# A decoder layer's feed-forward: the second matrix, too, by Strassen's seven block products

## The chip, the cores and the metric

The kernel runs on one core of a Trainium2 chip. TensorE (PE) multiplies matrices out of SBUF into PSUM, which has eight banks of 128 x 512 float32. VectorE (DVE) and ScalarE (ACT) read PSUM and SBUF, GpSimd (POOL) only SBUF. SyncE (SP) issues most of the DMAs. Each engine works through its own instructions in order and waits on semaphores for the others. The metric is device time in microseconds (us) of one execution.

## The reference

All arithmetic is float32. x is 8 x 256 x 1024, that is 2048 tokens of 1024.

```
x = x + selfattention(layernorm(x))          # 32 heads, sign weights
x = x + crossattention(layernorm(x), ctx)    # 16 heads
h = layernorm(x)
P = h @ U1                                   # 1024 -> 256
H = P @ V1 + b1                              # 256 -> 2 x 2752
act = silu(H[:, :2752]) * H[:, 2752:]
Z = act @ U2                                 # 2752 -> 256
x = x + Z @ V2 + b2                          # 256 -> 1024
```

The change concerns Z = act @ U2; its neighbours in the program are V1 and V2.

## The kernel before, in words

The two attentions take the first 960 us or so. Then comes the feed-forward, for two halves of 1024 tokens (`dbs`: d0, then d1). Each half has two column blocks of W = 512 tokens (t = 0, 1), and everything is held transposed, features on partitions. The instructions are issued in the order of the program on every engine; nothing reorders them.

`Head` prepares 512 tokens: it loads x rows from DRAM, normalizes them (`norm`), stores them, loads them back (`take`), transposes them on DVE (`turn`) and multiplies by U1 (`factor`, PSUM tile ps_p, copied out by ACT). `sums` forms four combinations t1 to t4 of a half's P blocks on DVE. Heads 0 and 1 (d0) come during the last cross attention; heads 2 and 3 (d1) during d0's units.

The 2752 hidden features are 21 full chunks of 128 and one of 64. `unit` (L1176) does one chunk for a whole half: gate and up parts of 128 features by two column blocks, that is a 2 x 2 by 2 x 2 block product, done with Strassen's seven products (Winograd's form) in place of eight. Its sums of V1 blocks (s_) come from `weight_sums` (L1151) on POOL, one unit ahead. The products go into three PSUM tiles, c21, c11 and c12. c21 gathers four products, and ACT copies it out between them (a1, q, q7). DVE adds and multiplies with scalar_tensor_tensor (`stt`), ACT takes the sigmoids, POOL does three multiplications. The results are g1 and ac2, the activations of that chunk for t = 0 and 1. The last steps of a unit (sigmoid sg2 and two POOL products, `rest`) are issued within the next unit, by `trailing`, and `mid` issues there what is due of other work (`todo`, filled by `at(unit, ...)`).

`down` (L1275) multiplies each chunk's activations by its rows of U2: four products of 128 x 128 by 128 x 512 per unit (two column blocks t, two halves r of the rank 256), all accumulated over the 21 chunks in four PSUM banks, zs (psA twice, psB, pso). They are queued in `zq` and `fill` puts them between the products of the next unit, as work that PE can do while it would wait. The 64-feature chunk is done by `half_unit` three units before the end, for both column blocks at once, and its U2 products by `across`. After the last chunk zs is copied to zT.

`tail` multiplies zT by V2 (PSUM tile ps_o, in two pieces of 512 columns per 128 tokens), adds the x rows on DVE and sends the result out; `tail_b` adds b2 to the x rows on POOL beforehand; `tail_x` loads them. The tail of d0 is spread over d1's units 1 to 8, that of d1 comes at the end. `tail_b` runs in d0's unit 20 and d1's units 1 to 7 for d0, and in d1's units 10 to 17 for d1.

The other four PSUM banks are one rotating pool, pss, which scores, c21, c11, c12, ps_h, ps_p of heads 2 and 3, and ps_o use.

## Time and profile before

| | |
|---|---|
| Median of 3 runs | 1477.05 us (1476.87 to 1477.11) |
| The profiled execution | 1477.6 us, its span 1475.8 us |
| PE busy | 1439.5 us, 98% of the span |
| DVE, ACT, POOL busy | 969.6, 853.1, 655.9 us |
| A unit of d0, from start to start | 9.52 us |
| The products c (L1189) | 588 records of 592 ns (634 for the fourth of c21), two to a product |
| The U2 products ps_z (L1285) | 336 records, 592 ns |
| POOL: L1231, L1232, L1215; L1156 to L1159; L1303 | 1.27 each; 0.455 each; 2.35 us |
| DVE: L1200, L1217, L1222, L1226; L1144; L1319 | 0.751 each; 0.692; 0.692 us |
| ACT: copies of c; sigmoids | 0.586; 0.63 us |

A line of the profile begins with a start and a duration, or with a source line. "c<-t,s_v" is an instruction that writes tile c from tiles t and s_v; buffer numbers are left out, so c21, c11 and c12 are all "c". PE records overlap: 592 ns is one from first to last element, and they start every 429 ns. PEld is the loading of weights. In square brackets stands how long an engine was idle before an instruction, and what ended that. In the row of slices each digit is the busy share of a fortieth of the span, in tenths.

### The profile page before, as it was taken

What the parts mean: (1) busy time and instruction counts of PE and PEld (TensorE: products, weight loads), DVE (VectorE), ACT (ScalarE), POOL (GpSimd) and SP (SyncE); (2) the same over time, 40 slices, a digit from 0 to 9 for tenths busy, and PEclk for the clock granted to TensorE, in tenths of its full rate; (3) what the DMA queues carried; (4) which work ended last, traced back from release to release, by engine and by line L of the source; (5) the groups of instructions that cost most, each with busy time, mean ns of one, the idle gap of its engine ahead of it and who ended that gap; (6) DMA issues with size and microseconds to landing.
All of it is one profiled execution on the core that took longest, in us unless ns stands there. A gap on an engine that the chain in (4) does not pass through costs nothing.

```text
span 1475.8 us, 25648 instructions
## 1 busy us (share of the span) xinstructions
PE 1439.5 (98%) x8986; PEld 960.4 (65%) x8986; DVE 969.6 (66%) x1894; ACT 853.1 (58%) x2557; POOL 655.9 (44%) x771
## 2 busy tenths in 40 slices
PE   6899999999999999989999999999999999999998
PEld 6778888888888887667777777644444344444433
DVE  6888898989898988767777777434424333333334
ACT  5778898989898988755555666433223222223320
POOL 2544444445454444312322264246645436657840
PEclk9999999999999999989999999999999999999999
DMA  8520020202020142344458674723212001230003
GB/s 230 114 58 17 29 71 18 73 16 73 16 73 21 39 131 93 115 118 131 133 149 281 203 226 148 224 72 121 86 43 89 25 1 61 82 125 33 0 0 114
DMA packets 102960, 134.74 MB, mean 91 GB/s; under 512 B 44538, under 2 KB 75440, under 8 KB 102704
## 3 DMA queue, kind: packets, MB, share of 16 engines
q1 hardware_dynamic: 98224, 116.33, 26.6%
q0 software_dynamic: 4608, 16.78, 2.9%
q8 instruction: 72, 1.18, 0.3%
q14 instruction: 56, 0.46, 0.1%
HBM read 90.60 MB, written 41.94 MB: 90 GB/s over the span
## 4 chain that ended last, share of the span: by engine, by line
PE 55%; ACT 2%; DVE 1%; DMA 1%; issue 0%; SPq 0%; ACTq 0%; DVEq 0%
PE c L1189 17%; PE ps_z L1285 10%; PE ps_pt L579 4%; PE s L676 4%; PE ps_o L1311 4%; PE ps_p L1123 4%; PE po L699 3%; PE ps_o L716 2%; PE ps_q L925 2%; PE ps_qk L941 2%; ACT p L762 2%; PE ps_k L855 1%; PE ps_o L547 1%; PE ps_h L1246 0%; DMA n<-xn 0%
## 5 line engine op out<-in xcount | busy, mean ns | idle before, releaser
L762 ACT ACTIVATE p<-s,nm 128x256 f32<-128x256 f32 x768 | 359.0, 519 | 3.3 <-DVE nm L743 3.3
L583 ACT COPY pT<-ps_pt 128x512 f32<-128x512 f32 x384 | 197.6, 599 | 145.9 <-PE ps_pt L579 145.8
L743 DVE TENSOR_REDUCE nm<-s 128x2 f32<-128x512 f32 x384 | 237.4, 678 | 5.2 <-PE s L676 3.7
L579 PE MATMUL ps_pt<-ident,p 128*128 128x128 f32 x1536 | 198.5, 281 | 5.9 <-DVE p L623 2.5
L579 PEld LDWEIGHTS ps_pt<-ident,p 128*128 128x128 f32 x1536 | 167.0, 142 | 46.5 <-issue 24.6
L762 ACT ACTIVATION_READ_ACCUMULATOR p<-s,nm 128x1 f32 x768 | 192.5, 251 | 0.0
L731 POOL TENSOR_TENSOR x1t<-x1t,y 128x256 f32<-128x256 f32 x64 | 46.3, 743 | 201.0 <-DVE y L724 201.0
L407 POOL TENSOR_SCALAR tmp<-y 128x512 f32<-128x512 f32 x78 | 58.5, 750 | 166.8 <-DVE y L556 91.6
L1217 DVE SCALAR_TENSOR_TENSOR ac<-c,b_col,q 128x512 f32<-128x512 f32 x42 | 31.5, 751 | 148.0 <-ACT q L1214 148.0
L1231 POOL TENSOR_TENSOR g<-g,sg 128x512 f32<-128x512 f32 x41 | 52.1, 1271 | 168.5 <-ACT sg L1230 168.5
L1195 ACT COPY a<-c 128x512 f32<-128x512 f32 x42 | 24.6, 586 | 169.1 <-PE c L1189 169.1
L1189 PE MATMUL c<-t,s_v 128*128 128x512 f32 x252 | 121.8, 592 | 0.0
L454 PE MATMUL ps_q<-xh,qT_w 128*128 128x256 f32 x496 | 121.8, 287 | 0.0
L454 PE MATMUL ps_q<-xl,qT_w 128*128 128x256 f32 x496 | 118.9, 281 | 0.0
L547 PE MATMUL ps_o<-oT_w,oh 128*128 128x512 f32 x256 | 106.5, 416 | 0.0
L547 PE MATMUL ps_o<-oT_w,ol 128*128 128x512 f32 x256 | 101.8, 398 | 0.0
L454 PEld LDWEIGHTS ps_q<-xh,qT_w 128*128 128x128 f32 x496 | 93.3, 188 | 1.7
L454 PEld LDWEIGHTS ps_q<-xl,qT_w 128*128 128x128 f32 x496 | 93.4, 188 | 0.0
L623 DVE TENSOR_SCALAR p<-p,sm 128x256 f32<-128x256 f32 x256 | 86.8, 396 | 8.4 <-PE ps_q L454 0.5
L630 ACT ACTIVATE p<-p,sm 128x256 f32<-128x256 f32 x172 | 75.9, 514 | 19.1 <-DVE sm L613 18.5
L1189 PEld LDWEIGHTS c<-t,s_v 128*128 128x128 f32 x252 | 47.7, 190 | 60.0 <-issue 57.6
L1285 PE MATMUL ps_z<-g,u_sb 128*128 128x512 f32 x168 | 85.3, 592 | 0.0
(185 smaller groups left out, 3038.2 us busy)
## 6 DMA issues: line engine op xcount, KB each, us to landing
xs<-in_x_dram SPq DMA_DIRECT2D x32, 512.0 KB
x<-xs POOLq DMA_DIRECT2D x16, 512.0 KB, 3.1
x1t<-x SPq DMA_DIRECT2D x16, 512.0 KB
c<-in_ctx_dram SPq DMA_DIRECT2D x64, 128.0 KB
n<-xn SPq DMA_DIRECT2D x32, 256.0 KB
xp<-n SPq DMA_DIRECT2D x64, 128.0 KB
x<-x1t POOLq DMA_DIRECT2D x16, 512.0 KB, 5.6
x2n<-x SPq DMA_DIRECT2D x16, 512.0 KB
```

What stands on the lines that cost most here:

```text
L454: nc.tensor.matmul(ps[:, i, :], w(i, e), x_[:, e, :], start=(e == 0 and x_ is st.xh), stop=(e == EC - 1 and x_ is st.xl),)
L547: nc.tensor.matmul(ps, o_[c // 4][:, c % 4, t * P : (t + 1) * P], oT_w[:, c, h * 512 : (h + 1) * 512], start=(c == 0 and o_ is st.oh), sto ...
L579: nc.tensor.transpose(ps[:, k, t * P : (t + 1) * P], p[:, t, k * P : (k + 1) * P], ident)
L583: nc.scalar.copy(pT, ps)
L623: nc.vector.tensor_scalar_mul(p, p, self.sm[:, t, j : j + 1])
L630: nc.scalar.activation(p, p, AF.Copy, scale=self.sm[:, t, j : j + 1])
L676: nc.tensor.matmul(s[2 * i + j][:, t, :], st.cqk[p0 : p0 + XD, 2 * c + i, t * P : (t + 1) * P], st.ckv[p0 : p0 + XD, :], start=True, stop= ...
L743: nc.vector.tensor_reduce(nm[:, j, :], s[j], AX.X, ALU.max, negate=True)
L762: nc.scalar.activation(cur.p[j][:, t, :], s[j][:, t, :], AF.Exp, bias=nm[:, j, t : t + 1], accum_out=cur.sm[:, t, j : j + 1],)
L1123: nc.tensor.matmul(ps, fw.u1[:, e, r * P : (r + 1) * P], self.chunk(e), start=(e == 0), stop=(e == EC - 1),)
L1189: nc.tensor.matmul(ps, w, x_, start=start, stop=stop, skip_group_check=True)
L1285: nc.tensor.matmul(db.zs[t][r], fw.u2[f // 4][:, f % 4, r * P : (r + 1) * P], ac, start=(k == 0), stop=last,)
```

## The change

Pairs of chunks (`pair`: chunks f1 and f2 of units 2p and 2p+1) form 2 x 2 blocks with the two column blocks and the two halves of the rank, and are multiplied with seven products (P1 to P7) in place of eight. Ten pairs cover 20 of the 21 chunks; the last one is multiplied as before (`left`). Four of the seven products are kept in PSUM over all pairs (keys "2", "3", "4" and "5" in the four banks that zs had). The other three (P1, P6, P7, key "1") go one after another into one bank, and DVE adds each to zT in SBUF (`more`). `finish` puts the sums together. DVE forms t1 and t2 (new tiles) and t3 and t4 (in place) from the activations; POOL forms four sums of U2 blocks in the place of zT[:, 0, 1, :] (`sums1`, `sums2`). A pair's products are issued in units 2p+2 (P1, P2, P5) and 2p+3 (P6, P3, P7, P4), at the places `jobs`, its other work at `also` and `sums_`.

The pool pss becomes four single banks with names of their own: c21 and c11 swap banks 0 and 1 from unit to unit (`flip`), c12 has bank 2, the key "1" tile bank 3. ps_p of heads 2 and 3 and the tails' first piece take the bank of the last c11 (`spare`), the tails' other pieces bank 2. Scratch tiles change their places. The last attention step's `weighted`, `early` and `late` move into d0's unit 0; `half_unit` moves from before unit 18 to before unit 20. Two norms and four turns of the heads now share a unit, on odd units; tails, their loads and `tail_b` move one or two units later.

```
-    pss = ctx.enter_context(tc.tile_pool(name="pss", bufs=4, space=PSUM))
+    pss = ctx.enter_context(tc.tile_pool(name="pss", bufs=1, space=PSUM))
...
-                ps = pss.tile([P, W], F32, tag="pss", name="ps_p")
+                ps = spare("ps_p")
...
+    def bank_(i, name):
+        return pss.tile([P, W], F32, tag=f"pss{i}", name=name)
+    def spare(name):
+        return bank_(1 - flip[0], name)
...
+        flip[0] ^= 1
+        c21 = bank_(flip[0], "c21")
         product(c21, v1_of(0, 0, f, P), b11, True, False)
         act(a1, c21)
+        c11 = bank_(1 - flip[0], "c11")
         product(c11, v1_of(1, 0, f, P), b21, True, True)
         trailing()
         stt(g1, c11, bg, a1, ALU.add, ALU.add)
         if mid is not None:
             mid()
-        fill(1 + (extra > 0))
+        do(jobs[0])
+        do(also[0])
         product(c21, s_[:, 1, :], db.t2, False, False)
         nc.scalar.activation(sg1, g1, AF.Sigmoid)
         act(q, c21)
+        c12 = bank_(2, "c12")
         product(c12, s_[:, 0, :], db.t1, True, False)
-        fill(1 + (extra > 1))
+        do(sums_[0])
+        do(jobs[1])
         product(c21, s_[:, 2, :], db.t3, False, False)
         act(q7, c21)
         mul(g1, g1, sg1)
         stt(ac2, c12, bu, q7, ALU.add, ALU.add)
         if following is not None:
             weight_sums(*following)
-        fill()
+        do(sums_[1])
+        do(jobs[2])
         product(c21, v1_of(1, 1, f, P), db.t4, False, True)
         stt(g1, c21, bu, g1, ALU.add, ALU.mult)
-        fill()
+        do(also[1])
+        do(jobs[3])
         product(c12, s_[:, 3, :], b22, False, True)
         stt(g2, c12, bg, q, ALU.add, ALU.add)
+        do(also[2])
...
+        def t1():
+            m.b11, m.b12 = db.ac[2 * p]
+            sub(m.t1, m.b12, m.b11)
+        def t23():
+            m.b21, m.b22 = db.ac[2 * p + 1]
+            sub(m.t2, m.b22, m.t1)
+            sub(m.b12, m.b22, m.b12)
+        def t4():
+            sub(m.b21, m.b21, m.t2)
+        def sums1():
+            m.s = db.zT[:, 0, 1, :].rearrange("p (k c) -> p k c", k=4)
+            nc.gpsimd.tensor_add(m.s[:, 0, :], u2_of(f1, 1), u2_of(f2, 1))
+        def sums2():
+            g.tensor_sub(m.s[:, 1, :], m.s[:, 0, :], u2_of(f1, 0))
+            g.tensor_sub(m.s[:, 3, :], u2_of(f2, 0), m.s[:, 1, :])
+            g.tensor_sub(m.s[:, 2, :], u2_of(f1, 0), u2_of(f1, 1))
+        def more(t, r):
+            dst = db.zT[:, t, r, :]
+            if p:
+                add(dst, db.X["1"], dst)
+            else:
+                nc.vector.tensor_copy(dst, db.X["1"])
+            if end and t:
+                add(dst, dst, db.zT[:, r, 0, :])
...
++        p1 = new(chain(lambda: u2_of(f1, 0), lambda: m.b11))
++        p2 = kept("2", lambda: u2_of(f2, 0), lambda: m.b21)
++        p5 = kept("5", lambda: m.s[:, 0, :], lambda: m.t1, end)
++        p6 = new(chain(lambda: m.s[:, 1, :], lambda: m.t2))
++        p3 = kept("3", lambda: m.s[:, 3, :], lambda: m.b22)
++        p7 = new(chain(lambda: m.s[:, 2, :], lambda: m.b12))
++        p4 = kept("4", lambda: u2_of(f2, 1), lambda: m.b21)
++        m.even = dict(jobs=([p1], [p2], [p5], []),
++            also=([lambda: more(0, 0), t23], [], [t4]), sums_=([sums1], [sums2]))
++        m.odd = dict(jobs=([p6], [p3], [p7, p4], []),
++            also=([lambda: more(1, 0)], [lambda: more(1, 1)], []))
...
+    def left(db, t, r):
+        down(db, KEYS[t, r], u2_of(units[FULL - 1], r), db.ac[FULL - 1][t], True)
+    def finish(db, *which):
+        for t, r in which:
+            if (t, r) == (0, 1):
+                add(z[0][1], db.X["4"], z[1][1])
+            else:
+                add(z[t][r], db.X[KEYS[t, r]], z[t][r])
+            if t:
+                add(z[t][r], db.X["5"], z[t][r])
...
-            ps = pss.tile([P, n], F32, tag="pss", name="ps_o")
+            ps = bank_((1 - flip[0], 2)[c0 // 512], "ps_o")[:, 0:n]
...
+            if k // 2 < FULL // 2:
+                a = e["also"]
+                e["also"] = (a[0] + [pairs[db.i, k // 2].t1_],) + tuple(a[1:])
...
         for j in range(1, 2 * BT):
-            at(j, tail_b, d0, j)
+            at(j + 1, tail_b, d0, j)
         for j in range(2 * BT):
-            at(2 * BT + j, last_x, j)
-            at(2 * BT + j + 2, tail_b, d1, j)
+            at(2 * BT + j + 2, last_x, j)
+            at(2 * BT + j + 4, tail_b, d1, j)
...
         trailing()
-        fill(2)
-        tail(d1, 0)
-        fill(len(zq))
-        for j in range(1, 2 * BT - 1):
+        end = pairs[1, FULL // 2 - 1].odd
+        for i in range(4):
+            for f in end["jobs"][i]:
+                f()
+            if i in (0, 2):
+                end["also"][i // 2][0]()
+        for c in range(2):
+            across(d1, c)
+        for t in range(2):
+            for r in range(RC):
+                left(d1, t, r)
+            finish(d1, *([(0, 0), (0, 1)] if t == 0 else [(1, 0), (1, 1)]))
+        for j in range(2 * BT - 1):
             tail(d1, j)
```

t1 of a pair is issued in unit 2p+1, at that unit's first `also` place. At d0's end `trailing`, P6 and its add come before the two factors of head 3; P3, P7 and P4 follow in d1's unit 0, and `across`, `left` and `finish` of d0 in d1's unit 1.

## The prediction

> **What bounds the kernel now.** I read the page's busy line first, then its slices, then the chain of waits in the feed-forward stage, and last the timeline of single units there.

> ```profile
> PE 1439.5 (98%) x8986; PEld 960.4 (65%) x8986; DVE 969.6 (66%) x1894; ACT 853.1 (58%) x2557; POOL 655.9 (44%) x771
> PE   6899999999999999989999999999999999999998
> POOL 2544444445454444312322264246645436657840
> ...
> by line: PE c L1189 48.0%; PE ps_z L1285 27.3%; PE ps_o L1311 14.0%; PE ps_p L1123 6.2%; PE ps_h L1246 1.8%; PE ps_z L1265 1.1%; DVE g L1226 0.2%; DVE g L1231 0.2%; DVE ac L1232 0.2%; ACT sg L1230 0.2%; DVE zT L1295 0.2%; DVE x2t L1319 0.1%
> 1116.50 0.94 PE c L1189 x2
> 1117.44 0.86 PE ps_z L1285 x2
> 1118.30 2.58 PE c L1189 x6
> ```

> PE never rests in the last 500 us: the chain there is PE work end to end. A matmul is two records of 0.429 us, so a product costs 0.857 us (a "slot"). A unit, from 1108.78 to 1118.30, takes 9.52 us: 7+4 slots are 9.43, and 0.09 is the 0.94 (for 0.86) of the fourth c21 product, which waits for the copy q7. So a slot removed is worth 0.857 us, if nothing that feeds PE comes later than before. What feeds it stands in one unit, which starts at 1366.46:

> ```profile
> 1366.46 1.02 PE L1189 MATMUL c<-pT,w_ffn 128*128 128x512 f32 x2
> 1367.52 0.59 ACT L1195 COPY a<-c 128x512 f32<-128x512 f32 x1 [3.79 <-PE c L1189]
> 1368.01 0.63 ACT L1230 ACTIVATE sg<-g 128x512 f32<-128x512 f32 x1
> 1368.71 1.27 POOL L1231 TENSOR_TENSOR g<-g,sg 128x512 f32<-128x512 f32 x1 [1.59 <-ACT sg L1230]
> 1370.06 1.27 POOL L1232 TENSOR_TENSOR ac<-ac,g 128x512 f32<-128x512 f32 x1
> 1371.29 2.36 POOL L1303 TENSOR_TENSOR x2t<-x2t,b_sb 128x1024 f32<-128x1024 f32 x1
> 1373.29 0.75 DVE L1217 SCALAR_TENSOR_TENSOR ac<-c,b_col,q 128x512 f32<-128x512 f32 x1 [4.09 <-ACT q L1214]
> 1373.59 1.28 POOL L1215 TENSOR_TENSOR g<-g,sg 128x512 f32<-128x512 f32 x1
> 1374.81 0.47 POOL L1156 TENSOR_TENSOR s_v<-w_ffn,v1b 128x128 f32<-128x128 f32 x1
> ```

> POOL starts 2.25 us into the unit, held by ACT (a, then sg); its two products of the unit before end at 4.83; the bias add of the tail (L1303, 2.35 us, in 16 units) ends at 7.13. Today nothing on PE waits for it.

> The next rows show what happens when DVE and POOL both work from SBUF:

> ```profile
> 966.48 0.99 DVE L1143 TENSOR_TENSOR t<-pT 128x512 f32<-128x512 f32 x1 [1.04 <-PE ps_p L1123]
> 966.88 0.90 POOL L1156 TENSOR_TENSOR s_v<-w_ffn,v1b 128x128 f32<-128x128 f32 x1
> ...
> 1433.33 0.69 DVE L1215 TENSOR_TENSOR g<-g,sg 128x512 f32<-128x512 f32 x1 [0.76 <-ACT sg L1206]
> 1433.43 1.71 POOL L1232 TENSOR_TENSOR ac<-ac,g 128x512 f32<-128x512 f32 x1
> 1443.14 3.70 PE L1311 MATMUL ps_o<-v_sb,zT 128*128 128x512 f32 x8 [1.90 <-DVE zT L1295]
> ```

> A DVE operation with two SBUF inputs and a POOL operation exclude each other: the subtraction of 966.48 took 0.99 (others 0.69), the POOL sum behind it 0.90 (others 0.455), and a POOL product of 1.27 took 1.71. The last line is PE's only real pause at the end, 1.90 us.

> **Gains.** (a) 10 pairs in each of two halves lose one product each: 20 x 0.857 = 17.1. (b) In odd units two products stand between q7's source and the fourth c21 product, so the 0.09 goes in 19 units (3 to 19 of each half, and d1's unit 1, which has z products there): 1.7. (c) In d0's unit 0 PE now has the 16 small matmuls of the last attention step between c11 and the next product, where it had a 0.68 pause; from the end of the factor (971.4) unit 0 takes about 9.0 where 10.05 passed until 981.42: 1.05. (d) The 1.90 pause above goes with the old end. Together 21.8.

> **What is added and hidden.** Three DVE adds from PSUM per pair (as L1319, 0.692) and four subtractions (as L1144, 0.692) are 4.9 us; DVE's four L1200/L1217/L1222/L1226 operations are 3.0 of 9.5 us a unit: room for them, if the moment suits. The four sums of u2 chunks on POOL (as L1156 to L1159, 0.455) are 1.8 us per pair. The reads of u2 chunks 4 and 5 and the loads of x rows move on SP behind unit 0 or by one unit: u2's are first used in unit 16, and each x row still has a unit or more between load and use. So nothing. Fixed banks for c21, c11, c12: each is read out 0.9 us or more before its next use. So nothing inside the units.

> **Losses.** In an even unit the slots start at: c21 0, c11 0.86, P1 1.71, c21 2.57, c12 3.43, P2 4.29, c21 5.14, P5 6.00, c21 6.86, c12 7.71, end 8.57 plus 0.09.

> 1. *P5 behind the bias add.* P5 needs the first u2 sum, which POOL's queue has behind the two products and, in 9 even units (d0's 20; d1's 2, 4, 6, 8, 12, 14, 16, 18), behind L1303. Without exclusion the sum ends at 7.13+0.46 = 7.59; PE follows a POOL result after 0 to 0.3 us (the handover is not shown cleanly; I take 0.27, as from the end of the POOL product at 980.30 to the matmul at 980.57): start 7.86 instead of 6.00, less the 0.09 that vanishes: 1.77 each, 15.9. With exclusion DVE's t2, which waits for the POOL product that ends at 4.87, asks at 4.90, just after L1303 has started; it runs 7.13 to 7.70, the sum 7.70 to 8.12, P5 at 8.4: 2.3, and 2.4 where an odd unit has left POOL late: 5 x 2.3 + 4 x 2.4 = 21.1.
> 2. *Odd units 13, 15, 17, 19 of d1.* POOL enters late (2.6 for 2.25), t1 waits for L1303's end (7.5), ac's scalar_tensor_tensor stands behind it on DVE, and the last c12 product behind that: 8.9 to 9.1 for 8.57. 0.5 each, 2.0; without exclusion 0. In d1's 3, 5, 7 the tail's 3.43 us of PE work let POOL catch up: 0.
> 3. *Even units without a bias add.* POOL: sum until 5.25, t2 until 5.80, then the product L1215, waiting since 5.25, until 7.03, then the next subtraction until 7.6; ac's operation ends 8.33 and the last c12 product starts 8.4 for 7.8: 0.6 in 8 units, 4.8. d0's unit 2 has inv_std (0.96) and two DMA issues (1.2 from 996.89 to 998.07) ahead of the sum: 1.7; unit 6 has inv_std (1.5): 1.1; d1's unit 20 has its products on DVE: 0.95. Together 8.55; without exclusion 2.0.
> 4. *Two norms (L1077) in one unit* (d0's 3, 5, 11, 13): each waits for a POOL product, as at 1102.60 (1.42), so the add that frees P7's bank ends at 6.55: P7 0.65 late, 2.6; with 0.55 each and no waiting 1.6. Two pairs of transposes (2.5) just fit: 0.
> 5. *Bank of the factor.* ps_p takes the bank that the next c21 (or the second factor) needs at once; ACT copies it out first: 0.2+0.59+0.05 = 0.85, four times: 3.4.
> 6. *d0's unit 1* has no product to fill: c21 waits for q (4.02 for 3.43) and q7 (5.73 for 4.88): 1.4.
> 7. *P6 behind d0's unit 20* waits for the second u2 sum, behind four sums of v1 chunks: 1.55; 1.0 without exclusion.
> 8. *End.* P7's bank waits for an add that DVE has behind sg2 and the two last products: start 13.3 us after unit 20's start for 11.3, 2.0. The last three pieces share one bank and wait for each other's add (0.65 and 0.5): 1.2. Together 3.2; the adds of z hide behind across and left (5.5 us).

> D1's unit 2 also has six adds of finish before its first DVE operation, but its P5 waits longer anyway.

> Losses 21.1+2.0+8.55+2.6+3.4+1.4+1.55+3.2 = 43.8; minus 21.8: 22 us slower. The profiled execution took 1477.6 (span 1475.8 and 1.8 around it), 0.04% above the median of 1477.05; I add to the median: 1499.

> [...]

> **Rivals.**
> - *No order from the exclusion* (subtractions slip in at no price): 15.9+0+2.0+1.6+3.4+1.4+1.0+3.2 = 28.5, minus 21.8: 1483.8. For it: only the few rows above and the norms show the wait. Against: each shows it.
> - *Worse queueing*: in units with a bias add, the POOL product overtakes the second subtraction as in step 3, so the last c12 product starts 0.7 later, 9 times, and odd units lose double (2 more): 1499+8.3 = 1507. The order at 8.12 decides it.
> - *Faster: the u2 sum is in time.* If P5 does not wait behind L1303, step 1 is 0; with the cheap values elsewhere 12.6 of losses against 21.8: 1468. It decides where P5's wait falls under 1.0 us in the nine units (9.2/9). Against it: POOL keeps its order, and in the rows above it is busy without a gap from 2.25 until past 7.13.

> **How the numbers follow.** 1499: 0.53; 1484: 0.21; 1507: 0.13; faster, about 1468: 0.13. The range 1481 to 1508 leaves out the last and the edges of the others. About 0.2% (3 us) is what a measurement of this kernel can tell from no change; 0.04 lies within it, at the near edge of the 1484 case: faster 0.13, same 0.04, slower 0.83. The likeliest case's own range is 1492 to 1505.

> **What would show it.** PE's weight load for P5 waiting for POOL sums in the nine units, about 2 us each; bias adds with DVE subtractions of 2 to 3 us beside them; ACT's ps_p copy releasing c21 four times; 20 products fewer (40 records); even units near 9.3 and odd near 9.4 where no bias add runs. Wrong if P5 has no wait, if even units run at 8.7, or if the end is waited out elsewhere.

## The result, and the profile after

| | before | after |
|---|---|---|
| Median, measured together | 1477.08 us (1476.87 to 1478.39) | 1496.98 us (1495.98 to 1497.75) |
| Ratio, 95% interval | | 1.0132 (1.0115 to 1.0150) |
| The profiled execution, its span | 1477.6, 1475.8 us | 1497.6, 1495.5 us |
| PE busy | 1439.5 us, 8986 matmul records | 1430.3 us, 8946 records |
| DVE, POOL busy | 969.6, 655.9 us | 1120.0, 723.3 us |
| Start of the last factor before d0's unit 0 (ps_p, 7.03 us) | 964.49 us | 960.77 us |
| From there to the end: "the stage" | 511.3 us | 534.7 us |

The change makes the kernel slower by 1.3%; 1499 was predicted. The instructions ahead of the stage are the same in both, yet they take between 960.8 and 965.2 us in the profiles of this case (the granted clock of TensorE stood at 0.92 to 0.97 between 600 and 700 us). So profiles are compared here by the stage: it takes 23.4 us more.

The page of the kernel after, its busy line and two rows of its slices (tenths of a fortieth of the span):

```profile
PE 1430.3 (96%) x8946; PEld 952.5 (64%) x8946; DVE 1120.0 (75%) x2046; ACT 849.6 (57%) x2553; POOL 723.3 (48%) x851
...
PE   7899999999999999899999999999999999998988
...
POOL 2544454445354534122232435177657646668950
```

The 40 records that are missing are the 20 products. PE is busy 9 us less, in a span 20 us longer; three of the last four slices show 8 tenths. Of DVE's 150 us more some 100 are the added instructions (4.9 us for each of 20 pairs); the rest is waiting that their records contain.

A unit with a bias add (d1's unit 12), in the timeline: start and duration in us, engine, line, operation, and in brackets the idle time before it and what ended that.

```profile
1352.56 1.02 PE L1189 MATMUL c<-pT,w_ffn 128*128 128x512 f32 x2
...
1356.22 1.27 POOL L1241 TENSOR_TENSOR ac<-ac,g 128x512 f32<-128x512 f32 x1
...
1357.44 2.35 POOL L1396 TENSOR_TENSOR x2t<-x2t,b_sb 128x1024 f32<-128x1024 f32 x1
1357.52 2.82 DVE L1302 TENSOR_TENSOR t<-ac,t 128x512 f32<-128x512 f32 x1 [1.50 <-POOL ac L1241]
...
1359.75 0.90 POOL L1310 TENSOR_TENSOR zT<-u_sb 128x128 f32<-128x128 f32 x1
1360.26 0.93 DVE L1303 TENSOR_TENSOR ac<-ac,ac 128x512 f32<-128x512 f32 x1
1360.61 1.71 POOL L1221 TENSOR_TENSOR g<-g,sg 128x512 f32<-128x512 f32 x1
...
1360.70 1.13 PE L1285 MATMUL z<-t,zT 128*128 128x512 f32 x2 [1.98 <-POOL zT L1310]
1361.12 0.74 DVE L1223 SCALAR_TENSOR_TENSOR ac<-c,b_col,q 128x512 f32<-128x512 f32 x1
```

Read it downwards: the bias add (L1396) starts as the second product (L1241) ends. DVE's t2 (L1302) asks 0.08 us later, and its record lasts 2.82 us, for 0.69 of work: it gets its turn when the bias add ends. Then POOL's first u2 sum (L1310) has its turn, then DVE's second subtraction (L1303), then POOL's product: they alternate, one operation each. P5 (the z of 1360.70) starts 0.05 us after the sum's end and 8.14 us into the unit, where its place is 6.00. PE had nothing for 1.98 us.

An even unit without a bias add (d0's 14):

```profile
1121.70 0.93 DVE L1302 TENSOR_TENSOR t<-ac,t 128x512 f32<-128x512 f32 x1 [1.50 <-POOL ac L1241]
...
1122.04 1.72 POOL L1221 TENSOR_TENSOR g<-g,sg 128x512 f32<-128x512 f32 x1
1122.55 1.75 DVE L1303 TENSOR_TENSOR ac<-ac,ac 128x512 f32<-128x512 f32 x1
...
1124.22 0.74 DVE L1223 SCALAR_TENSOR_TENSOR ac<-c,b_col,q 128x512 f32<-128x512 f32 x1
...
1125.02 1.13 PE L1189 MATMUL c<-pT,s_v 128*128 128x512 f32 x2 [0.31 <-DVE ac L1223]
```

The second subtraction waits for the POOL product beside it (1.75 us for 0.69), ac's operation stands behind it, and the last c12 product behind that: 9.24 us from unit start to unit start, for 8.66.

Something else took time that no step of the prediction has. The same d1 unit and its successor by stretches of 2 us; the columns are the busy time (and instructions) of PE, PEld, DVE, ACT and POOL, then the granted clock of TensorE:

```profile
1358.00:1360.00 2.00, 0.73 (x2) 0.00 (x0) 2.00 (x1) 0.58 (x1) 2.00 (x2) 1.00 0.00 0
1360.00:1362.00 2.00, 1.30 (x3) 0.68 (x4) 1.86 (x3) 0.00 (x0) 2.00 (x2) 1.00 0.00 0
1362.00:1364.00 2.00, 2.00 (x4) 0.80 (x3) 0.66 (x1) 0.00 (x0) 1.92 (x5) 0.50 0.00 0
1364.00:1366.00 2.00, 2.00 (x5) 0.81 (x4) 1.11 (x3) 0.00 (x0) 1.37 (x4) 0.65 0.00 0
```

Behind P5's wait the clock is halved for 3.4 us, and PE loses 1.7 us more: d1's unit 18, which holds such a stretch whole, takes 12.51 us where units 14 and 16 take 10.82. This document calls such a stretch a clock dip. There are three in this profile, each behind one of its ten waits of 1.76 to 1.99 us: 5.1 us.

### The profile page after: what moved, and what is told of

Read it like the earlier page. It is cut to its first block, busy times and chain, and to the rows that moved or that the text cites. A ratio compares the mean times of both kernels' runs of the same rounds, so it can differ in the third digit from the quotient of the medians.

```text
span 1495.5 us, 25859 instructions
## 1 busy us (share of the span) xinstructions
PE 1430.3 (96%) x8946; PEld 952.5 (64%) x8946; DVE 1120.0 (75%) x2046; ACT 849.6 (57%) x2553; POOL 723.3 (48%) x851
## 4 chain that ended last, share of the span: by engine, by line
PE 44%; POOL 6%; DVE 4%; ACT 3%; issue 2%; DMA 1%; SPq 0%; ACTq 0%; DVEq 0%; POOLq 0%
PE c L1189 11%; PE z L1285 6%; PE ps_pt L579 4%; PE ps_o L1404 4%; PE s L676 4%; PE ps_p L1123 4%; PE po L699 3%; PE ps_o L716 2%; PE ps_q L925 2%; PE ps_qk L941 2%; POOL g L1240 2%; POOL ac L1241 2%; ACT p L762 2%; POOL x2t L1396 1%; PE ps_k L855 1%
## 5 line engine op out<-in xcount | busy, mean ns | idle before, releaser
L1189 PE MATMUL c<-t,s_v 128*128 128x512 f32 x252 | 122.2, 594 | 1.2 <-ACT q L1213 1.2
L1240 POOL TENSOR_TENSOR g<-g,sg 128x512 f32<-128x512 f32 x41 | 52.2, 1273 | 115.4 <-ACT sg L1239 115.4
L1189 PEld LDWEIGHTS c<-t,s_v 128*128 128x128 f32 x252 | 47.4, 190 | 62.7 <-issue 51.6
L600 PE MATMUL s<-kT,qT 32*128 32x256 f32 x1024 | 75.9, 401 | 3.8 <-DVE qT L412 2.4
L1221 POOL TENSOR_TENSOR g<-g,sg 128x512 f32<-128x512 f32 x41 | 64.5, 1573 | 22.3 <-ACT sg L1211 22.3
```

The lines of the kernel that those rows point to most:

```text
L600: nc.tensor.matmul(s[j][:, t, :], st.qT[p0 : p0 + 32, c, t * P : (t + 1) * P], st.kT[p0 : p0 + 32, c // 4, :], start=True, stop=True,)
L1189: nc.tensor.matmul(ps, w, x_, start=start, stop=stop, skip_group_check=True)
L1240: mul(g2, g2, sg2)
```

## The experiments

The theory is the prediction's: POOL works in the order of its queue, and a DVE operation with two SBUF inputs and a POOL operation take turns (2.82 us for t2's 0.69 above); the losses are the eight steps, and they add up. The rivals say that only POOL's order matters, that only POOL's and DVE's load does, or that the waits hide one another. All ratios are against the kernel before, with 95% intervals; "net" is the stage of the profile less 1.7 us for each clock dip that PE worked through, an estimate from the 1.69 of that unit 18. The changed kernel's net is 529.6 us, the kernel before's 511.3.

| kernel | median us | ratio | stage us | dips | net us |
|---|---|---|---|---|---|
| changed | 1496.98 | 1.0132 (1.0115 to 1.0150) | 534.7 | 3 | 529.6 |
| sum first | 1499.35 | 1.0151 (1.0136 to 1.0166) | 531.9 | 1 | 530.2 |
| bias add last | 1486.02 | 1.0061 (1.0044 to 1.0078) | 520.4 | 1 | 518.7 |
| second subtraction later | 1492.21 | 1.0102 (1.0086 to 1.0119) | 526.5 | 1 | 524.8 |
| transposes for subtractions | 1483.66 | 1.0050 (1.0035 to 1.0065) | 520.4 | 0 | 520.4 |
| banks and end | 1493.62 | 1.0109 (1.0094 to 1.0124) | 527.0 | 2 | 523.6 |
| waits filled | 1495.05 | 1.0118 (1.0102 to 1.0133) | 530.8 | 0 | 530.8 |
| five edits | 1472.35 | 0.9965 (0.9953 to 0.9978) | 506.6 | 0 | 506.6 |
| eight edits | 1466.68 | 0.9926 (0.9913 to 0.9938) | 500.9 | 0 | 500.9 |
| and bias adds spread | 1463.11 | 0.9917 (0.9903 to 0.9930) | 499.3 | 0 | 499.3 |
| and t2 later | 1475.46 | 0.9994 (0.9985 to 1.0003) | 512.6 | 2 | 509.2 |

**The u2 sum first.** Only the place of one POOL instruction changes.

```
         product(c11, v1_of(1, 0, f, P), b21, True, True)
+        do(sums_[0])
         trailing()
...
-        do(sums_[0])
         do(jobs[1])
```

> POOL's first sum of u2 chunks is issued ahead of the two products, so that it can no longer stand behind the bias add; nothing else changes. Theory (exclusion and order of the queue): P5 starts on time in all even units, but in the nine with a bias add the DVE subtraction t2 still waits for the bias add's end (7.2 us into the unit, so t2 runs until 7.8), the POOL product then goes ahead of the second subtraction (until 9.05), that one ends at 9.7, ac's scalar_tensor_tensor at 10.45, and the last c12 product starts at 10.5: a unit of about 11.3 in place of 10.7. The wait moves from P5 to the last c12 product and grows; time about 1502 (1497 to 1504). Rival (the place of the sum in POOL's queue is the whole cost): the 9 waits of 2.0 go, about 1479.

Measured: 1499.35. The same unit (starting at 1354.2 here), in the timeline of this kernel:

```profile
1359.11 2.35 POOL L1400 TENSOR_TENSOR x2t<-x2t,b_sb 128x1024 f32<-128x1024 f32 x1
1359.18 2.83 DVE L1302 TENSOR_TENSOR t<-ac,t 128x512 f32<-128x512 f32 x1 [1.49 <-POOL ac L1241]
1361.41 1.72 POOL L1221 TENSOR_TENSOR g<-g,sg 128x512 f32<-128x512 f32 x1
1361.93 1.75 DVE L1303 TENSOR_TENSOR ac<-ac,ac 128x512 f32<-128x512 f32 x1
...
1363.60 0.74 DVE L1223 SCALAR_TENSOR_TENSOR ac<-c,b_col,q 128x512 f32<-128x512 f32 x1
...
1364.39 2.00 PE L1189 MATMUL c<-pT,s_v 128*128 128x512 f32 x2 [2.20 <-DVE ac L1223]
```

P5 has no wait. The last c12 product now waits 2.20 us, at the end of a row of four turns: bias add, t2, product, second subtraction. The rival's 1479 is out. The gain where POOL's sum alone was late (d0's units 2 and 6, P6 after d0's unit 20) is some 2.2 us and almost makes up for the longer units (11.13 us for 10.82, where about 11.3 was expected): net 0.6 us more, not 5.

**The bias add last.** The instruction that holds the turn longest goes behind all of POOL's other work of its unit.

```
         do(sums_[1])
+        do(late)
         do(jobs[2])
...
-        at(20, tail_b, d0, 0)
+        biases = {(0, 20): lambda: tail_b(d0, 0)}
...
-            at(j + 1, tail_b, d0, j)
+            biases[1, j + 1] = lambda j=j: tail_b(d0, j)
...
-            at(2 * BT + j + 4, tail_b, d1, j)
+            biases[1, 2 * BT + j + 4] = lambda j=j: tail_b(d1, j)
...
+                late=[biases[1, k]] if (1, k) in biases else (),
```

> The bias add (tail_b) is issued last on POOL within its unit, behind the product, the four sums of v1 chunks and the three sums of u2 chunks; nothing else changes. Theory: in the nine even units the wait falls from 2.03 to the 0.55 of the other even units, 13.3 us less; POOL comes about 1.2 us later into the odd units, whose t1 is then late, which may give back up to 0.7 in each of 8 (5.6). The clock dips after these waits should go with them (about 4). 1480 to 1489, 1484 taken. Rival (the bias add is not the cause, PE waits for the sum for another reason): no change, 1497. Rival (POOL's load is the cause, whatever its order): odd units lose what even ones gain, 1494 or more.

Measured: 1486.02, net 10.9 us less than the changed kernel. Timeline of d1's unit 13, an odd one, that starts at 1356.8:

```profile
1358.60 2.36 POOL L1397 TENSOR_TENSOR x2t<-x2t,b_sb 128x1024 f32<-128x1024 f32 x1
...
1360.92 1.27 POOL L1241 TENSOR_TENSOR g<-g,sg 128x512 f32<-128x512 f32 x1
...
1363.56 1.74 DVE L1298 TENSOR_TENSOR t<-ac,g 128x512 f32<-128x512 f32 x1 [3.32 <-POOL ac L1242]
...
1366.02 1.12 PE L1189 MATMUL c<-pT,s_v 128*128 128x512 f32 x2 [0.50 <-DVE ac L1223]
```

The even units fall to the 0.55 of the others, as expected. The bias add of the even unit is done only 4.2 us into the odd one, POOL's products start late, t1 (L1298) gets its turn behind the next product, and the last c12 product of the odd unit waits 0.50. Such units take 10.2 us for 9.44: a give-back of 0.8 in four odd units, where up to 0.7 in eight was allowed for. So the place of the bias add was the cause of the largest loss; and even with that mended the changed kernel is slower than the kernel before.

**The second subtraction later.**

```
             sub(m.t2, m.b22, m.t1)
+        def t3():
             sub(m.b12, m.b22, m.b12)
...
-            sums_=([sums1], [sums2]),
+            sums_=([sums1], [sums2, t3]),
```

> The second subtraction of an even unit (b22 - b12, needed only by P7 in the next unit) is issued behind ac's scalar_tensor_tensor on DVE in place of ahead of it; nothing else changes. Theory (exclusion: it waits for a whole POOL product and holds up ac's operation, and so the last c12 product): the 0.55 of each of 8 even units and the like in d0's unit 6 and d1's unit 20 go, P5's waits of 2.03 stay: about 1492. Rival (ac's operation is late because DVE is busy there anyway): the 0.55 stays, 1497.

Measured: 1492.21, net 4.8 less. Timeline of d1's unit 12:

```profile
1358.41 0.74 DVE L1223 SCALAR_TENSOR_TENSOR ac<-c,b_col,q 128x512 f32<-128x512 f32 x1
...
1358.85 1.13 PE L1285 MATMUL z<-t,zT 128*128 128x512 f32 x2 [1.97 <-POOL zT L1312]
1359.07 1.50 DVE L1305 TENSOR_TENSOR ac<-ac,ac 128x512 f32<-128x512 f32 x1
```

ac's operation comes before the subtraction that waits (1.50 us), and no even unit of this profile has a wait at its last c12 product. P5's 1.97 is untouched. The two losses are separate.

**No exclusion.** The subtractions are left out, and transposes of the same size, which read one tile, stand in their places.

```
-            sub(m.t1, m.b12, m.b11)
+            nc.vector.transpose(m.t1, m.b12)
-            sub(m.t2, m.b22, m.t1)
-            sub(m.b12, m.b22, m.b12)
+            nc.vector.transpose(m.t2, m.b22)
+            nc.vector.transpose(m.b12, m.b22)
-            sub(m.b21, m.b21, m.t2)
+            nc.vector.transpose(m.b21, m.t2)
```

> The four subtractions of a pair (t1, t2, t3, t4) are replaced by DVE transposes of the same size and length, which read one tile (the transposes of the heads show no stretch beside POOL: 0.67 us in the middle, 0.71 at most). The subtractions themselves are left out. Theory (two-input DVE operations and POOL exclude each other): t2 no longer waits for the bias add, the sum behind it takes 0.46 in place of 0.90 and P5 starts at about 7.75 in place of 8.14 (9 x 0.4 = 3.6); the 0.55 in 8 even units and the like in d0's 6 and d1's 20 go (5 to 6): about 1487. The rest of P5's wait, 1.6, stays, as it comes from the order of POOL's queue. Rival (no exclusion, the waits come from DVE's and POOL's load alone): no change, 1497. Rival (all of P5's wait is exclusion): 1497 - 18 - 6, about 1473.

Measured: 1483.66. Timeline of d1's unit 12:

```profile
1351.03 2.35 POOL L1396 TENSOR_TENSOR x2t<-x2t,b_sb 128x1024 f32<-128x1024 f32 x1
1351.74 0.67 DVE L1303 STREAM_TRANSPOSE ac<-ac 128x512 f32<-128x512 f32 x1
...
1353.33 0.46 POOL L1310 TENSOR_TENSOR zT<-u_sb 128x128 f32<-128x128 f32 x1
...
1353.85 1.12 PE L1285 MATMUL z<-t,zT 128*128 128x512 f32 x2 [1.54 <-POOL zT L1310]
```

The transpose takes its 0.67 us in the midst of the bias add, the sum takes 0.46 in place of 0.90, and PE waits 1.54 in place of 1.98: of P5's wait 0.44 was exclusion and the rest POOL's order. The 0.55 of the even units is gone. Net 9.2 us less, where 10 was expected; one wait grew: d0's unit 5, in which the two norms ahead of the add that frees P7's bank now take 3.54 us for 2.55, is 1.3 us longer. This is the prediction's rival "no order from the exclusion" made real; it gave 1483.8 for it. Beside the bias add the transpose, which reads one tile, takes 0.67 us; the subtraction t2 of the changed kernel, which reads two, takes 2.82.

**Banks and end** (steps 5 and 8).

```
-                ps = spare("ps_p")
+                ps = bank_(flip[0], "ps_p") if last else spare("ps_p")
...
-                h2.factor(k - 10)
+                h2.factor(k - 10, True)
...
-        h3.factor(1)
+        h3.factor(1, True)
...
-        trailing()
         end = pairs[1, FULL // 2 - 1].odd
         for i in range(4):
...
                 end["also"][i // 2][0]()
+            if i == 0:
+                trailing()
...
+            if apart and c0 > 512:
+                i = flip[0] if c0 < 896 else 3
```

> Three edits that touch steps 5 and 8 alone: the factors of heads 2 and the second of head 3 go into the bank of the c21 just finished, not the one that the next c21 needs at once; at the end P6 and the add that frees P7's bank go ahead of the last unit's sigmoid and products on DVE; the last two pieces have banks of their own. Theory: 4 x 0.85 = 3.4, P7's 2.0 and some 0.6 to 1.2 of the last pieces go, and at times a clock dip of 1.7 behind P7's wait: 1490 (1488 to 1492). Rival (these waits are covered by later ones): 1497.

Measured: 1493.62, above the 1488 to 1492 that was expected, and the interval overlaps that of the changed kernel; but two of this profile's P5 waits had a clock dip behind them, and net it is 6.0 us less. The changed kernel's PE rows after a factor and at P7:

```profile
1079.59 1.12 PE L1189 MATMUL c<-pT,w_ffn 128*128 128x512 f32 x2 [0.68 <-ACT pT L1130]
...
1454.10 1.99 PE L1285 MATMUL z<-ac,zT 128*128 128x512 f32 x2 [1.99 <-DVE zT L1330]
```

and the same two here:

```profile
1081.11 1.02 PE L1189 MATMUL c<-pT,w_ffn 128*128 128x512 f32 x2
...
1450.97 1.10 PE L1285 MATMUL z<-ac,zT 128*128 128x512 f32 x2 [0.42 <-DVE zT L1330]
```

By unit lengths some 3.4 of the 6.0 us come from the factors, which is all of step 5. The end gives only 1.8, where at least 2.6 was expected: P7's wait is 0.42, and the last pieces' waits of 0.52 and 0.38 are gone, but not all of that time is won. Another 1.2 is P6's wait behind d0's unit 20, which was covered by the clock dip ahead of it and not by an edit.

**The waits filled.** This one is about the clock.

```
+        def spin():
+            w, x_ = u2_of(f1, 0), m.b11
+            ps = bank_(3, "spin")
+            for _ in range(2):
+                nc.tensor.matmul(ps, w, x_, start=True, stop=True, skip_group_check=True)
...
+        biased = p == FULL // 2 - 1 if db.i == 0 else 0 < p < FULL // 2 - 1
...
-            jobs=([p1], [p2], [p5], []),
+            jobs=([p1], [p2], [spin, p5] if biased else [p5], []),
```

The same two matmuls stand ahead of P7 at the end. For d1 `biased` takes in pairs 1 to 8, and so unit 10, too, which has neither a bias add nor such a wait. So there are ten places and not nine, and 20 products more than in the changed kernel (40 records), 17.1 us of PE work, where the expectation counts 18 and 15.4.

> Nine of PE's waits of 2 us (P5's in the eight even units of d0's 20 and d1's 4 to 18, P7's at the end) are filled with two matmuls of a product's size each, whose results nobody reads: 18 products more than the changed kernel, 15.4 us of PE work. The waits themselves end when they did. Question: the profiles of the changed kernel and of the moved sum showed the granted clock at 0.5 for 3.41 us after some waits of 2 us (three and one of them), 1.7 us lost each. Theory: the dip follows from PE standing still, and comes where the whole wait lies within one window of 3.41 us (the dips of the changed kernel start 61.45 and 30.72 us apart, 18 and 9 times 3.41). Then it is gone, and the kernel with more work is faster: 1497 less 4 to 7, about 1492, with a clock of 1.00 from the feed-forward's start until the last pieces. Rival (the dips come from something else): about 1497 with dips. Rival (the matmuls are not hidden): up to 1512.

Measured: 1495.05. The wait of d1's unit 12 in the timeline, then the stretches:

```profile
1361.95 1.88 PE L1355 MATMUL spin<-g,u_sb 128*128 128x512 f32 x4
1364.10 1.12 PE L1285 MATMUL z<-t,zT 128*128 128x512 f32 x2 [0.27 <-POOL zT L1310]
```

```profile
1364.00:1366.00 2.00, 1.90 (x5) 0.94 (x6) 1.26 (x2) 0.00 (x0) 2.00 (x3) 1.00 0.00 0
1366.00:1368.00 2.00, 2.00 (x6) 0.88 (x5) 1.76 (x3) 0.10 (x1) 1.84 (x6) 1.00 0.00 0
```

The clock is 1.00 throughout the stage, until PE's work is over, and the stage is 3.9 us shorter than the changed kernel's with 17.1 us more work on PE: 5.1 us of dips are gone, and 1.2 were lost. Of these, 1.06 is d1's unit 10 (10.30 us for 9.24), where no wait covers the matmuls; in the nine waits they were hidden (10.84 us for 10.82). One profile without dips could be luck, as others have only one. But the mean clock of a whole execution is 0.993 to 0.997 in the four executions of this kernel, and 0.992 or 0.993 in the four of the changed one. By the times the gain is 1.9 us, and the intervals overlap: the effect on the clock is shown, its worth in an average execution isn't settled.

**Five edits together**: sum first, bias add last, second subtraction later, banks, end.

> Five edits together: bias add last on POOL in its unit, second subtraction behind ac's operation, first u2 sum ahead of POOL's two products, banks of the factors, order and banks of the end. Theory (the waits are separate and add up): 1497 - 11 (bias add, as measured) - 0.46 x 18 (the last c12 product in all even units) - 2.2 (d0's units 2 and 6, P6) - 7 (banks and end) = 1469 (1465 to 1473), faster than before the change. Rival (POOL and DVE are then too full and the waits return in other places, as in four odd units already when the bias add was moved): 1477 or more.

Measured: 1472.35, ratio 0.9965. The separate net gains add up to 2.2 (the sum's part that was not given back) + 10.9 + 4.8 + 6.0 = 23.9, and the 0.57 that the moved bias add had left in eight even units (4.6) would make it 28.5, with P6's wait counted twice in it; the stage is net 23.0 shorter. The rival was right in part: POOL falls behind in d1's last units, and the last c12 product waits 0.68 to 0.99 in four odd ones (13, 15, 17 and 19), which makes them 4.7 us longer. That of unit 15:

```profile
1377.68 1.13 PE L1189 MATMUL c<-pT,s_v 128*128 128x512 f32 x2 [0.99 <-DVE ac L1223]
```

**Eight edits.** t1 goes behind ac's operation, the norms behind the add that frees P7's bank, and three of the six adds of finish into d1's unit 2.

```
-                e["also"] = (a[0] + [pairs[db.i, k // 2].t1_],) + tuple(a[1:])
+                e["sums_"] = ([], [pairs[db.i, k // 2].t1_])
...
         do(also[0])
+        if then is not None:
+            then()
...
-            also=(e1["also"][0], [], [lambda: finish(d0, (0, 1), (1, 1), (0, 0), (1, 0))]),
+            also=(e1["also"][0], [], [lambda: finish(d0, (0, 1), (1, 1))]),
+        two["also"] = ([lambda: finish(d0, (0, 0), (1, 0))] + two["also"][0], *two["also"][1:])
```

> As the kernel with five edits, and three more: t1 (odd units) behind ac's operation, the two norms of a unit behind the add that frees P7's bank, and half of the six adds of finish moved from d1's unit 1 into its unit 2. Theory: 0.57 in four odd units, 0.54 in four units with norms and about 1.2 in d1's unit 2 go: 1469 - 5.6 = 1463. Rival (the room on DVE is used up): 1469 or more.

Measured: 1466.68. The stage is 5.6 us shorter, as expected, though not all of it where expected. The four units with norms are 2.5 us shorter together, d1's unit 2 is 1.2 shorter and d0's unit 1 0.6. The last c12 product no longer waits in the four odd units (4.7), but the wait comes back, smaller, in the even ones behind three of them: 0.75 to 1.08 in units 14, 16 and 18 (3.4). That of unit 16:

```profile
1378.79 1.12 PE L1189 MATMUL c<-pT,s_v 128*128 128x512 f32 x2 [1.07 <-DVE ac L1225]
```

**Bias adds spread.**

```
-            at(2 * BT + j + 2, last_x, j)
-            biases[1, 2 * BT + j + 4] = lambda j=j: tail_b(d1, j)
+            k = (9, 10, 11, 13, 14, 16, 17, 19)[j]
+            at(k - 2, last_x, j)
+            biases[1, k] = lambda j=j: tail_b(d1, j)
```

> As the kernel with eight edits; the bias adds of d1's rows, which stand in units 12 to 19 without a break, are spread over units 9, 10, 11, 13, 14, 16, 17 and 19 (their loads two units ahead of each). Theory: with a bias add in every unit POOL has more to do than a pair of units lasts (17.9 us for 17.3), so it falls behind, and the last c12 product waits 0.99 to 1.32 in three even units; with breaks it catches up: 1466.7 - 3.3 = 1463.4 (1461 to 1465). Rival (these waits have another cause): 1467.

Measured: 1463.11, the fastest; the stage is 1.6 us shorter, where 3.3 was expected. Units 14 and 16 have no wait left. Unit 18 still waits 0.77, and unit 12 now waits 0.76; each has bias adds in both of the units before it, and that of the odd one runs into the even unit, whose products are late for it. The intervals of this kernel and the one with eight edits overlap, so the last step is shown by the profile alone. Its busy line and row of PE:

```profile
PE 1421.3 (97%) x8946; PEld 953.1 (65%) x8946; DVE 1092.8 (75%) x2046; ACT 849.5 (58%) x2553; POOL 726.9 (50%) x851
...
PE   6899999999999999989999999999999999999999
```

**t2 later as well.**

```
-            also=([lambda: more(0, 0), t23], [], [t4]),
-            sums_=([sums1], [sums2, t3]),
+            also=([blocks, lambda: more(0, 0)], [], [t3, t4]),
+            sums_=([sums1], [sums2, t23]),
```

(`blocks` only names the two tiles early.)

> As the spread one, and t2 of even units is issued behind ac's operation too, with the second subtraction behind the unit's last scalar_tensor_tensor, so that nothing with two SBUF inputs stands ahead of ac's operation on DVE. Theory: what is left of the waits of the last c12 product goes; it can't be more than e9 leaves, so 1463 or up to 1 us less. Rival (the subtractions now meet the bias add, 2.35 us, and hold up DVE's work for the next unit): 1466 or more.

Measured: 1475.46, 12 us slower than without it. Timeline around the start of an odd unit of d1:

```profile
1328.20 2.36 POOL L1407 TENSOR_TENSOR x2t<-x2t,b_sb 128x1024 f32<-128x1024 f32 x1
1328.23 2.88 DVE L1310 TENSOR_TENSOR ac<-ac,ac 128x512 f32<-128x512 f32 x1
...
1332.71 0.74 DVE L1205 SCALAR_TENSOR_TENSOR g<-c,b_col,a 128x512 f32<-128x512 f32 x1
...
1333.54 0.63 ACT L1214 ACTIVATE sg<-g 128x512 f32<-128x512 f32 x1 [4.13 <-DVE g L1205]
1334.07 0.57 ACT L1216 COPY q<-c 128x512 f32<-128x512 f32 x1
...
1334.69 1.59 PE L1189 MATMUL c<-t,s_v 128*128 128x512 f32 x2 [2.20 <-ACT q L1216]
```

The subtraction meets the bias add by 0.03 us and waits it out; DVE's first operation of the next unit (L1205), ACT's sigmoid, ACT's copy q behind it, and c21's third product come late in a row. It is the rival's case. There are three waits of 2.20 (units 11, 15 and 17), two of them with a clock dip behind, and units 6 and 8, with tails, are 1.7 us longer each.

## Why the prediction was right, step by step

The measured sizes are differences of unit lengths (8.66 for an even unit without loss, 9.43 for an odd one) or gaps of PE.

| step | predicted us | measured us |
|---|---|---|
| gains (a) to (d) | 21.8 | 21.7 |
| 1 P5 behind the bias add | 21.1 | 19.5 (9 x 2.16) |
| 2 odd units of d1 | 2.0 | 0.4 |
| 3 even units without bias add | 8.55 | 7.8 |
| 4 two norms in a unit | 2.6 | 2.6 |
| 5 bank of the factor | 3.4 | 3.4 |
| 6 d0's unit 1 | 1.4 | 2.2 |
| 7 P6 behind d0's unit 20 | 1.55 | 1.2 |
| 8 end | 3.2 | 3.3 |
| sum of losses | 43.8 | 40.4 |
| clock dips | not foreseen | 5.1 |
| net | 22.0 | 23.8; the stage 23.4 |

*Gains.* The 40 records are gone, odd units without other work take 9.44 and not 9.53, d0's unit 0 gives 0.9 for 1.05, the pause of 1.90 is gone.

*Step 1* has its mechanism and its order of turns, which the alternation in the first timeline shows, and the moved bias add and the transposes confirm in two parts. That a subtraction waits out a whole POOL operation was the author's estimate, from a few rows of before; in the runs its 0.69 us become 2.82 beside the bias add and 1.75 beside a POOL product. What was mis-sized is the handover from POOL to PE: 0.27 was taken, 0.05 measured. The row that the 0.27 came from doesn't show it cleanly: the product before the matmul of 980.57 started at 979.60 and takes 0.86, so that matmul had its place at 980.46 anyway. d1's unit 2 was predicted to lose as much as the others for P5 alone; it does lose 2.18, but in three pieces, the two larger ones from the six adds of finish that were put at nothing there; with the bias add moved away it still loses 1.86.

*Step 2* is the term that missed by most in proportion: 0.5 per unit was predicted for POOL entering late and t1 standing behind the bias add; 0.1 was measured. The chain of waits is there, but it starts earlier: in d1's unit 15 POOL starts 2.36 us into the unit and the bias add ends at 7.30, where 2.6 and 7.5 were taken. The likely reason, argued and not tested, is that the even unit's own delay of 2.1 us lets POOL catch up before the odd one.

*Step 3*: 0.57 for 0.6 in eight units; taking the second subtraction out of the path, or the exclusion, removes just that. d0's unit 2 was 1.95 for 1.7 and its unit 6 0.74 for 1.1.

*Steps 4, 5 and 8* came out as worked, by the waits in the profile; when the end's waits were removed, only 1.8 of step 8's 3.3 us were won. *Step 6* missed one wait: behind q and q7, the last c12 product, too, waits 0.68 for ac's operation, which stands behind t1.

*The rivals.* "No order from the exclusion" has what it needs to happen in the kernel with transposes, and is there 1483.66 for 1483.8; but that closeness is luck in part: the norms keep their exclusion there (the two of d0's unit 5 take 3.54 us), and its stage is 9.1 us longer than that of the kernel before, not 6.7, which the shorter part ahead of the stage (961.1 us for 964.5) makes up for. "Worse queueing" did not happen: in units with a bias add the second subtraction gets its turn ahead of the product (1360.26 and 1360.61 in the first timeline). "The u2 sum is in time" was to decide it if P5's wait fell under 1.0 us: with the sum first it fell to nothing and the kernel was no faster, since t2 has the bias add ahead of it just the same. The rival's error was to price only P5.

So the sum of 1499 is close to 1497 partly by compensation: losses 3.4 us too large, against clock dips of 5.1 that it does not have, and the part ahead of the stage, which was 3.7 us shorter in this profile than in that of before. What stays open is how much the dips cost in an average execution, and whether the part ahead of the stage, whose length differs by up to 4.4 us among the profiles of this case, is shorter by more than chance.

## What to carry to other kernels

A product saved on PE is worth its time only while the engines that feed it stay off its path: 17 us of products were saved, and 40 us of waits came with them. Of these, 30 went (net 529.6 to 499.3) by giving instructions of 0.5 to 2.4 us another place in their queues, and some products other banks. Before moving work to DVE and POOL, look for the longest POOL instruction and for what it will stand in front of, in POOL's own queue and, where DVE reads two SBUF tiles, in DVE's (t2's 2.82 us for 0.69); then put ahead what PE needs soon and behind it what is only needed a unit later. With that mended the same arithmetic is 0.8% faster than the kernel before (0.9917, 0.9903 to 0.9930) in place of 1.3% slower.

## What the runs showed of the hardware that was not expected

A wait of 2 us of PE cost 3.7 where a dip followed it (1.97 and the 1.69 above in d1's unit 18). Which wait has a dip behind it differs among the profiles: d1's unit 12 has one in the changed kernel and with the sum first, and none with the second subtraction later.
